# A macaron block on one core: f16 projections, stores of scores merged in pairs and issued from ACT's queue, q and k stored in one piece

## The chip, the core and the metric

The kernel runs on one core of a Trainium2 chip. The metric is the device time of one execution in microseconds (us); lower is better. A core has TensorE (PE; PEld is its loading of weights), VectorE (DVE), ScalarE (ACT), GpSimd (POOL) and SyncE (SP). Each engine carries out its instructions in the order of the program. Transfers (DMAs) are issued by an engine's queue, here that of SyncE or of ACT, and land later. "Activation" in a listing is ACT.

## What is computed

x has 8 sequences of 1024 tokens with 256 channels. Three sublayers follow one another, each with a layer norm in front and a residual:

```
x = x + 0.5 * ffn(layernorm(x))
x = x + attention(layernorm(x))
x = x + 0.5 * ffn(layernorm(x))

ffn(x):   xr, xk = mu * x + (1 - mu) * x_prev          # x_prev: the token before
          sigmoid(xr @ W_r.T) * (relu(xk @ W_k.T)**2 @ W_v.T)

attention(x), 16 heads of 16, 40 offsets o (0 to 32, 48, 64, 96, 128, 192, 256, 384):
          logit_o = (q . k shifted by o) / 4 * (1 + q . scale_o) + bias_o     # masked where t < o
          p = softmax over the offsets; out = sum over o of p_o * (v shifted by o)
          (out * gain * sigmoid(x @ gate_w.T + gate_b)) @ out_w.T + out_b
```

## The kernel before

The work is cut into five stages, written as Python generators in `macaron`: the first FFN (`stage_f1`), the projections q, k, v and gate (`stage_p`), the scores (`stage_qk`), softmax and the sum over v (`stage_att`), and the second FFN (`stage_f2`). The FFNs and projections go by 32 chunks of 256 tokens, the scores by 16 half batches of 512 tokens (four steps each), attention by 64 tiles of 128 tokens. A list of steps at the end of the function orders the stages by hand (line 520, with the offsets TRACE and RANK); within these priorities a scheduler, when the kernel is built, fixes one order of instructions for each engine. Each DMA is given one of eight completion semaphores in rotation, and is issued only when the last DMA on that semaphore has landed, if that isn't known already.

**Projections (lines 233 to 295).** The normalized chunk is transposed on TensorE and split into a high and a low part (xh, xl, lines 244 and 245), as are the weights (wa_hi, wa_lo, lines 97 to 99), all in the type F32R. Each product is three matmuls: high x high, high x low, low x high. There are 1536 of them, of 256 columns each, 48 a chunk. For q and k, ACT writes the f16 high part of the result into hl (line 263) and VectorE the low part (line 264). hl goes to DRAM twice (line 270), since the score matmul contracts over four stacked pieces: q as high, low, high, low and k as high, high, low, low. That is 2 DMAs for each of 128 tiles of hl.

**Scores (lines 297 to 367).** q and k come back from DRAM as qst and kb (lines 317 and 319). `scores` multiplies them into one PSUM bank and ACT copies the bank to SBUF, into a tile called sl (line 308). *Far* tiles, for offsets over 32, come first: two in an even half batch, four in an odd one. They go to the DRAM buffer sf (line 346), four DMAs a tile. Then come four *local* tiles, which go to the DRAM buffer of the half batch, again four DMAs a tile (line 362). In all that makes 192 + 256 = 448 DMAs of about 128 KB, from 112 tiles. The SBUF tiles come from a pool of two. All these DMAs are issued by SyncE.

**Attention (lines 369 to 506).** SyncE loads a tile's local scores from DRAM with a skew, so that each token's 33 offsets lie side by side, into lg (line 377), and the far ones into ef (line 379). VectorE multiplies them with 1 + q . scale (lines 405 and 410; the product gp is in PSUM), POOL adds the bias (line 419), ACT takes the exponential (line 425). ACT's queue stores the probabilities to DRAM (line 426), and SyncE loads them back unskewed into pd (line 428). pd is transposed on TensorE (line 464), copied to ptt by ACT (line 470) and multiplied with v.

Of the kernel before, what the change touches and what calls it, by code (L numbers as in the profile page):

```python
# [7 lines left out]

F32 = mybir.dt.float32
F32R = mybir.dt.float32r  # L10
F16 = mybir.dt.float16
I32 = mybir.dt.int32
AF = mybir.ActivationFunctionType
ALU = mybir.AluOpType
# [11 lines left out]
NL = LW + 1  # L26
# [6 lines left out]
ROW = 1024  # L33
# [4 lines left out]
VPAD = 96  # L38
VROW = 2 * 8 * 17
F2A = 28  # L40
TRACE = (0, 3.6, -4.4, -8.1, -10.6)
RANK = (0, 5.1, -4.4, -8.1, -10.6)

# [6 lines left out]
def macaron(ctx: ExitStack, tc: tile.TileContext, x, wffn, watt, wo, cols, rows, pbias, se, mask, out):  # L50
# [13 lines left out]
    bv, bo = row[:, 0], row[:, 1]  # L64
    bias = const.tile([128, NO * 16], F32, name="bias")
    msk = const.tile([128, 3, NO], F32, name="msk")
    wa_hi = const.tile([128, 4, 2, 256], F32R, name="wa_hi")
    wa_lo = const.tile([128, 4, 2, 256], F32R, name="wa_lo")
    seb = const.tile([128, 2, NO], F16, name="seb")
    half = const.tile([128, 4], F32, name="half")  # L70
    nc.gpsimd.memset(half, -0.5)
# [21 lines left out]
    def load_att():  # L93
        with tc.tile_pool(name="setup", bufs=1) as sp:
            wst = sp.tile([128, 4, 2, 256], F32, name="wst")
            nc.sync.dma_start(wst, watt.rearrange("w (c p) d -> p w c d", p=128))
            nc.vector.tensor_scalar(wst[:, 0], wst[:, 0], 0.25, None, ALU.mult)
            nc.vector.tensor_copy(wa_hi, wst)
            nc.vector.tensor_tensor(wa_lo, wst, wa_hi.bitcast(F32), ALU.subtract)
            nc.vector.tensor_scalar(b_q, b_q, 0.25, None, ALU.mult)  # L100
            nc.vector.tensor_scalar(b_g, b_g, 0.5, None, ALU.mult)
            nc.sync.dma_start(row, rows.unsqueeze(0).to_broadcast([128, 2, 256]))
            for t in [t.bitcast(F32) for t in kb] + vw:
                nc.gpsimd.memset(t, 0.0)
            zero = kb[1].bitcast(F32).rearrange("p a b w -> p (a b w)")
            for i in range(2):
                nc.sync.dma_start(v_d[i][0 : VPAD * VROW].rearrange("(p w) -> p w", p=VPAD), zero[:VPAD, :VROW])
            nc.sync.dma_start(sf_d[0:PADF].rearrange("(p w) -> p w", p=16), zero[:16, : PADF // 16])
            for c0, c1, w in ((0, 8, 384), (8, 15, 384), (15, 16, 368)):
                o = PADF + c0 * ROW + ROW - 384  # L110
                nc.sync.dma_start(flat(sf_d, o, (SF_T, 32), (ROW, c1 - c0), (1, w)), zero[:32, : (c1 - c0) * w])
            nc.sync.dma_start(flat(pd_d, NL * 16, (4 * SKEW, 128), (SKEW, 4), (1, SKEW - NL * 16)), zero[:, : 4 * 512])
            nc.sync.dma_start(bias, pbias.to_broadcast([128, NO * 16]))
            nc.sync.dma_start(msk, mask.rearrange("t p u -> p t u"))
            nc.sync.dma_start(wot, wo.rearrange("(c p) d -> p c d", p=128))
            for c in range(2):
                nc.vector.tensor_scalar(wot[:, c], wot[:, c], gain[:, c : c + 1], 0.5, ALU.mult, ALU.mult)
# [115 lines left out]
    def stage_p():  # L233
        for c in range(NCH):
# [7 lines left out]
            xh = pw.tile([128, 2, 256], F32R, name="xh", tag="xk" + s)  # L242
            xl = pw.tile([128, 2, 256], F32R, name="xl", tag="xr" + s)
            nc.scalar.copy(xh, tr)
            nc.vector.tensor_tensor(xl, tr, xh.bitcast(F32), ALU.subtract)

            def proj(w):
                p = ps.tile([128, 2, 256], F32, name="p", tag="ps" + s)
# [9 lines left out]

            for j, bb in ((0, b_q), (1, b_k)):
                p = proj(j)  # L260
                for g in range(2):
                    hl = pw.tile([128, 2, 256], F16, name="hl", bufs=4)
                    nc.scalar.activation(hl[:, 0], p[:, g], AF.Identity, bias=bb[:, g : g + 1])  # L263
                    nc.vector.scalar_tensor_tensor(  # L264
                        hl[:, 1], p[:, g], bb[:, g : g + 1], hl[:, 0], ALU.add, ALU.subtract
                    )
                    o = g * 128 * 2048 + cq * 256
                    for r in range(2):
                        ro, s2 = (r * 1024, 512) if j == 0 else (r * 512, 1024)
                        nc.sync.dma_start(flat(qk_d[i % 2][j], o + ro, (2048, 128), (s2, 2), (1, 256)), hl)  # L270
            p = proj(3)
            for g in range(2):
                nc.scalar.activation(gt[:, g], p[:, g], AF.Tanh, bias=b_g[:, g : g + 1], scale=0.5)
# [23 lines left out]
    def stage_qk():  # L297
        def scores(o, g, q4, q, k, keys):

            p = ps.tile([128, 512], F32, name="p", tag="psq")  # L300
            for pr in range(4):
                for s in range(len(q4(0))):
                    for a in range(4):
                        pp = p[32 * a : 32 * a + 32, pr * 128 : pr * 128 + 128].rearrange("n (h j) -> n h j", h=2)
                        w = 64 // len(q4(a))
                        ms = q4(a)[s]
                        mm(pp[:, :, s * w : s * w + w], q[:, pr, ms], k[:, pr, :, keys(ms)], True, True)
            nc.scalar.copy(o[:, :, :, g], p.rearrange("n (q h j) -> n j h q", q=4, h=2))  # L308

        for i in range(2 * B):  # L310
            hf = i % 2
# [11 lines left out]
            ns = 2 - hf  # L323
            nth = 4 // ns
            for th in range(nth):
                sf = psb.tile([128, 64, 2, 2, 4], F32, name="sl")
                for g in range(2):
                    scores(
                        sf,
                        g,  # L330
                        lambda a: [slice(c, 512, 16) for c in range((4 * th + a) * ns, (4 * th + a + 1) * ns)],
                        qs[i, g],
                        kb[g],
                        lambda ms: slice(LW + ms.start, LW + (hf + 1) * 512, 16),
                    )
                for a in range(4):
                    c = (4 * th + a) * ns
                    o = PADF + hf * 32 * SF_T + c * ROW
                    src = sf[32 * a : 32 * a + 32].rearrange("n j h g q -> n (j h g q)")
                    if hf == 0:  # L340
                        dst = flat(far, o, (SF_T, 32), (ROW, 2), (1, 512))
                        src = src.rearrange("n (s w) -> n s w", s=2)
                    else:
                        w = ROW - 16 if c == 15 else ROW
                        dst, src = flat(far, o, (SF_T, 32), (1, w)), src[:, :w]
                    nc.sync.dma_start(dst, src)
                if 2 * th + 2 == nth:
                    yield
            yield
            for t in range(4):  # L350
                sl = psb.tile([128, 64, 2, 2, 4], F32, name="sl")
                for g in range(2):
                    scores(
                        sl,
                        g,
                        lambda a: [slice(t * 128 + 32 * a, t * 128 + 32 * a + 32)],
                        qs[i, g],
                        kb[g],
                        lambda ms: slice(hf * 512 + ms.start, hf * 512 + ms.start + 64),
                    )  # L360
                for a in range(4):
                    nc.sync.dma_start(
                        flat(sl_d[i % 2], (4 * t + a) * BLK, (ROW, 32), (1, ROW)),
                        sl[32 * a : 32 * a + 32].rearrange("n j h g q -> n (j h g q)"),
                    )
                if t % 2:
                    yield

    def stage_att():
        for tt in range(B * NT):  # L370
# [27 lines left out]
            for h2 in range(2):  # L398
                gp = ps.tile([128, 64, 8], F32, name="gp")
                for g in range(2):  # L400
# [2 lines left out]
                        mm(gp[:, 0:NO, 4 * g + pr], q, seb[:, h2], True, True)  # L403
                e = slice(8 * h2, 8 * h2 + 8)
                nc.vector.scalar_tensor_tensor(
                    lg[:, 0:NL, e], gp[:, 0:NL], 1.0, lg[:, 0:NL, e], ALU.add, ALU.mult
                )
                for k0, k1 in FARG:
                    w0, w1 = (24 - FAR[k] // 16 for k in (k0, k1 - 1))
                    nc.vector.scalar_tensor_tensor(  # L410
                        lf[:, k0:k1, e],
                        gp[:, NL + k0 : NL + k1],
                        1.0,
                        ef[:, w0 : w1 + 1 : (w1 - w0) // (k1 - k0 - 1), e],
                        ALU.add,
                        ALU.mult,
# [169 lines left out]
```

## Time and profile before

| | us |
|---|---|
| median of 3 runs | 1260.52 (1255.84 to 1267.22) |
| the profiled execution, its own time | 1256.76 |
| its span, first to last instruction | 1254.0 |
| TensorE busy | 1089.2 |
| VectorE busy | 942.6 |
| GpSimd busy | 766.5 |
| ScalarE busy | 538.0 |

The profile is of one execution. Its page gives the busy time of each engine, then the chain of work that ended last, followed back from the last instruction, with the share of each engine and line in it, then groups of instructions by line, and the DMA issues. Further views list who waited for whom, the instructions of one line, and the instructions in order of time. "SPq" and "ACTq" are the instruction sequencers that issue DMAs; their work isn't counted as busy. A row such as `sl<-p` names the tile written and the tiles read. The granted clock of TensorE was 0.956 of full speed over the span. The sixteen DMA engines moved 282.88 MB at a mean of 226 GB/s.

### The profile page before, as it was taken

Reading aid. Unit: us, or ns where it says so; the run is one execution under the profiler, and the core shown is the slowest. Engines: PE = TensorE matmul, PEld = TensorE weight load, DVE = VectorE, ACT = ScalarE, POOL = GpSimd, SP = SyncE. Lnnn points to the kernel's source line nnn. Section 1 sums busy time; section 2 is a strip of 40 time slices with the busy share of each in tenths; the row PEclk is TensorE's granted clock in tenths of the full one; section 3 lists DMA queues with packets and bytes.
Section 4 is the critical chain, followed back from the end, with each engine's and each line's share of the span. In section 5 each row is a group of like instructions: output and inputs, shape, how many; then the busy total and the mean of one; then the engine's idle time right before and its main releaser. Section 6 shows DMA issues by size and latency. Waiting matters only on the chain.

```text
span 1254.0 us, 34712 instructions
## 1 busy us (share of the span) xinstructions
PE 1089.2 (87%) x13568; PEld 885.7 (71%) x13568; DVE 942.6 (75%) x2266; ACT 538.0 (43%) x1025; POOL 766.5 (61%) x1101
## 2 busy tenths in 40 slices
PE   2887989899799898989899989899988998888785
PEld 2676768677687677777777778786777787665664
DVE  7546768987587888879678866978858887877772
ACT  2444445344453444536345454544534444524231
POOL 7436619675575656659457564867656755657672
PEclk9999999899999999899999999999989999998988
DMA  8187888786878779787788977797787868998630
GB/s 263 32 224 222 241 242 265 229 238 194 251 226 254 230 233 274 221 252 232 193 260 257 254 201 230 228 269 227 233 243 234 269 197 254 284 280 265 202 99 24
DMA packets 256500, 282.88 MB, mean 226 GB/s; under 512 B 23440, under 2 KB 214608, under 8 KB 256336
## 3 DMA queue, kind: packets, MB, share of 16 engines
q1 hardware_dynamic: 247120, 263.36, 71.7%
q10 hardware_dynamic: 9216, 17.31, 3.8%
q8 instruction: 106, 1.74, 0.6%
q14 instruction: 58, 0.48, 0.1%
HBM read 151.67 MB, written 128.91 MB: 224 GB/s over the span
## 4 chain that ended last, share of the span: by engine, by line
PE 42%; DMA 25%; DVE 14%; SPq 6%; POOL 5%; issue 5%; ACT 4%; POOLq 0%; ACTq 0%; DVEq 0%
PE p L134 29%; DMA pd<-pd 9%; PE tra L464 4%; PE pv L134 3%; PE tra L134 3%; POOL prod L445 2%; DMA lg<-sl 2%; DMA x<-in_x_dram 2%; DMA qk<-hl 2%; DMA kb<-qk 2%; DMA sl<-sl 2%; DVE prod L457 2%; DVE xk L196 1%; PE gp L134 1%; DVE mx L423 1%
## 5 line engine op out<-in xcount | busy, mean ns | idle before, releaser
L134 PEld LDWEIGHTS <-qst 128*32 128x32 f16 (+1 forms) x5120 | 157.2, 120 | 100.1 <-issue 63.5
L134 PE MATMUL p<-kb,qst 128*32 128x128 f16 (+1 forms) x4096 | 185.1, 297 | 12.7 <-ACT sl L308 8.6
L308 ACT COPY sl<-p 128x512 f32<-128x512 f32 x224 | 130.8, 584 | 144.2 <-PE p L134 123.0
L445 POOL TENSOR_TENSOR prod<-v,lg 128x256 f32<-128x256 f32 x248 | 165.5, 687 | 10.2 <-ACT lg L425 6.1
L134 PE MATMUL p<-xk,w_f 128*128 128x256 f32 x512 | 144.9, 421 | 20.0 <-DVE xk L196 11.7
L419 POOL TENSOR_TENSOR lg<-lg,bias 128x640 f32<-128x640 f32 x64 | 113.5, 1774 | 71.8 <-DVE lg L410 66.9
L213 POOL TENSOR_TENSOR x<-x,xr 128x512 f32<-128x512 f32 x64 | 88.4, 1382 | 109.0 <-DVE xr L212 94.9
L457 DVE TENSOR_TENSOR prod<-prod 128x512 f32<-128x512 f32 (+2 forms) x120 | 126.1, 1051 | 32.1 <-POOL prod L445 31.5
L464 PE MATMUL tra<-ident,pd 128*128 128x128 f32 x512 | 97.1, 313 | 58.3 <-DMA pd<-pd 54.9
L160 ACT ACTIVATE xn<-x,nb,y 128x256 f32<-128x256 f32 x192 | 110.8, 602 | 63.0 <-DVE nb L152 55.2
L134 PE MATMUL p<-w_f,xk 128*128 128x256 f32 x512 | 132.9, 400 | 1.7 <-ACT xr L206 1.3
L134 PE MATMUL p<-w_f,xr 128*128 128x256 f32 x512 | 130.4, 396 | 3.6 <-ACT xk L201 2.8
L445 POOL TENSOR_TENSOR prod<-vn,lg 128x256 f32<-128x256 f32 x144 | 96.0, 678 | 54.3 <-ACT lg L425 35.4
L134 PE MATMUL p<-xh,wa_hi 128*128 128x256 f32 x384 | 123.2, 321 | 5.6 <-DVE hl L264 4.4
L134 PEld LDWEIGHTS p<-xk,w_f 128*128 128x128 f32 x512 | 99.3, 208 | 39.8 <-issue 10.5
L470 ACT COPY ptt<-tra 128x512 f32<-128x512 f32 x128 | 74.9, 585 | 116.1 <-PE tra L464 113.0
L464 PEld LDWEIGHTS tra<-ident,pd 128*128 128x128 f32 x512 | 71.0, 197 | 73.9 <-DMA pd<-pd 68.0
L263 ACT ACTIVATE hl<-p,col 128x256 f16<-128x256 f32 x128 | 60.6, 474 | 121.1 <-PE p L134 68.6
L134 PE MATMUL p<-xh,wa_lo 128*128 128x256 f32 x384 | 111.5, 290 | 0.0
L134 PE MATMUL p<-xl,wa_hi 128*128 128x256 f32 x384 | 111.4, 290 | 0.0
L134 PEld LDWEIGHTS p<-w_f,xr 128*128 128x128 f32 x512 | 95.3, 196 | 19.4 <-ACT xk L201 5.8
L134 PEld LDWEIGHTS p<-w_f,xk 128*128 128x128 f32 x512 | 96.0, 198 | 15.9 <-issue 2.8
(82 smaller groups left out, 2394.2 us busy)
## 6 DMA issues: line engine op xcount, KB each, us to landing
qk<-hl SPq DMA_DIRECT2D x256, 128.0 KB, 3.4
sl<-sl SPq DMA_DIRECT2D x256, 128.0 KB, 3.8
pd<-pd SPq DMA_DIRECT2D x64, 512.0 KB, 4.8
sf<-sl SPq DMA_DIRECT2D x184, 128.0 KB, 3.1
vw<-vd SPq DMA_DIRECT2D x128, 136.0 KB, 4.1
v<-vd SPq DMA_DIRECT2D x64, 272.0 KB, 4.3
lg<-sl SPq DMA_DIRECT2D x64, 264.0 KB, 4.1
pd<-lg ACTq DMA_DIRECT2D x64, 264.0 KB, 3.8
```

Source lines behind the costliest of these rows:

```text
L134: nc.tensor.matmul(o, l, r, start=start, stop=stop)
L160: nc.scalar.activation(xn, x2[:, i], AF.Identity, bias=nb[:, k : k + 1], scale=y[:, k : k + 1])
L196: nc.vector.scalar_tensor_tensor(o[:, h], xr[:, h], mu[:, h : h + 1], prev[:, h], ALU.mult, ALU.add)
L213: nc.gpsimd.tensor_tensor(x2, x2, xr, ALU.add)
L263: nc.scalar.activation(hl[:, 0], p[:, g], AF.Identity, bias=bb[:, g : g + 1])
L308: nc.scalar.copy(o[:, :, :, g], p.rearrange("n (q h j) -> n j h q", q=4, h=2))
L419: nc.gpsimd.tensor_tensor(la, la, bias, ALU.add)
L423: nc.vector.tensor_reduce(mx, lg.rearrange("p u e -> p e u"), AX.X, ALU.max)
L445: nc.gpsimd.tensor_tensor(prod[:, k], shifted[k][1]()[:, :, 0:16], lf[:, k].unsqueeze(2).to_broadcast([128, 16, 16]), ALU.mult,)
L457: nc.vector.tensor_tensor(o, terms[:, 0:m], terms[:, n - m : n], ALU.add)
L464: nc.tensor.transpose(tr[:, pr * 128 : pr * 128 + 128], pd.rearrange("p (m e) -> p m e", e=8)[:, :, 4 * g + pr], ident,)
L470: nc.scalar.copy(ptt.rearrange("p q n -> p (q n)"), tr)
```

## The change

There are four parts.

1. xh, xl, wa_hi and wa_lo become f16. The weights and the biases of q, k and v are scaled by WS = 16 (the bias of the gate isn't), and the scale is taken out later: in the copy of the scores (WS**-3), in 1 + q . scale (which becomes WS + ...), in the gate's tanh, and in the output weights. The cast to wa_hi moves from VectorE to ACT.
2. hl holds each tile of q or k with its copies, four pieces of 256. ACT and VectorE write each part twice in one instruction that reads the PSUM operand twice, and one DMA stores all of it: 128 DMAs in place of 256. The pool has two of these tiles in place of four of half the size.
3. Two tiles of scores share one SBUF tile of twice the size, and are stored together by four DMAs of about 256 KB after the second: 224 DMAs in place of 448. Which columns a far tile takes is rearranged to fit. In an even half batch, both far tiles are now made in the first of the four steps.
4. These 224 DMAs are issued by ACT's queue in place of SyncE's.

The core of the diff:

```diff
-    wa_hi = const.tile([128, 4, 2, 256], F32R, name="wa_hi")
-    wa_lo = const.tile([128, 4, 2, 256], F32R, name="wa_lo")
+    wa_hi = const.tile([128, 4, 2, 256], F16, name="wa_hi")
+    wa_lo = const.tile([128, 4, 2, 256], F16, name="wa_lo")
...
-            nc.vector.tensor_scalar(wst[:, 0], wst[:, 0], 0.25, None, ALU.mult)
-            nc.vector.tensor_copy(wa_hi, wst)
-            nc.vector.tensor_tensor(wa_lo, wst, wa_hi.bitcast(F32), ALU.subtract)
-            nc.vector.tensor_scalar(b_q, b_q, 0.25, None, ALU.mult)
+            nc.vector.tensor_scalar(wst[:, 0], wst[:, 0], 0.25 * WS, None, ALU.mult)
+            nc.vector.tensor_scalar(wst[:, 1:4], wst[:, 1:4], WS, None, ALU.mult)
+            nc.scalar.copy(wa_hi, wst)
+            nc.vector.tensor_tensor(wa_lo, wst, wa_hi, ALU.subtract)
+            nc.vector.tensor_scalar(b_q, b_q, 0.25 * WS, None, ALU.mult)
+            nc.vector.tensor_scalar(b_k, b_k, WS, None, ALU.mult)
...
+            nc.vector.tensor_scalar(bv, bv, WS, None, ALU.mult)
...
-                    hl = pw.tile([128, 2, 256], F16, name="hl", bufs=4)
-                    nc.scalar.activation(hl[:, 0], p[:, g], AF.Identity, bias=bb[:, g : g + 1])
-                    nc.vector.scalar_tensor_tensor(
-                        hl[:, 1], p[:, g], bb[:, g : g + 1], hl[:, 0], ALU.add, ALU.subtract
-                    )
-                    o = g * 128 * 2048 + cq * 256
-                    for r in range(2):
-                        ro, s2 = (r * 1024, 512) if j == 0 else (r * 512, 1024)
-                        nc.sync.dma_start(flat(qk_d[i % 2][j], o + ro, (2048, 128), (s2, 2), (1, 256)), hl)
+                    hl = pw.tile([128, 2, 2, 256], F16, name="hl", bufs=2)
+                    hi, lo = (hl[:, :, 0], hl[:, :, 1]) if j == 0 else (hl[:, 0], hl[:, 1])
+                    pp = p[:, g : g + 1].to_broadcast([128, 2, 256])
+                    nc.scalar.activation(hi, pp, AF.Identity, bias=bb[:, g : g + 1])
+                    nc.vector.scalar_tensor_tensor(lo, pp, bb[:, g : g + 1], hi, ALU.add, ALU.subtract)
+                    nc.sync.dma_start(
+                        flat(qk_d[i % 2][j], g * 128 * 2048 + cq * 256, (2048, 128), (512, 4), (1, 256)),
+                        hl.rearrange("p a b n -> p (a b) n"),
+                    )
...
-            nc.scalar.copy(o[:, :, :, g], p.rearrange("n (q h j) -> n j h q", q=4, h=2))
+            nc.scalar.mul(o[:, :, :, g], p.rearrange("n (q h j) -> n j h q", q=4, h=2), WS**-3)
...
-                sf = psb.tile([128, 64, 2, 2, 4], F32, name="sl")
+                if th % 2 == 0:
+                    sf = psb.tile([128, 2, 64, 2, 2, 4], F32, name="sl")
...
+                if th % 2 == 0:
+                    continue
...
                     if hf == 0:
-                        dst = flat(far, o, (SF_T, 32), (ROW, 2), (1, 512))
-                        src = src.rearrange("n (s w) -> n s w", s=2)
+                        dst = flat(far, o, (SF_T, 32), (ROW, 4), (1, 512))
+                        src = src.rearrange("n t (s w) -> n (t s) w", s=2)
                     else:
-                        w = ROW - 16 if c == 15 else ROW
-                        dst, src = flat(far, o, (SF_T, 32), (1, w)), src[:, :w]
-                    nc.sync.dma_start(dst, src)
-                if 2 * th + 2 == nth:
+                        dst, src = flat(far, o, (SF_T, 32), (ROW, 2), (1, ROW - 16)), src[:, :, : ROW - 16]
+                    nc.scalar.dma_start(dst, src)
+                if hf and th == 1:
                     yield
+            if not hf:
+                yield
             yield
...
-                sl = psb.tile([128, 64, 2, 2, 4], F32, name="sl")
+                if t % 2 == 0:
+                    sl = psb.tile([128, 2, 64, 2, 2, 4], F32, name="sl")
...
+                if t % 2 == 0:
+                    continue
                 for a in range(4):
-                    nc.sync.dma_start(
-                        flat(sl_d[i % 2], (4 * t + a) * BLK, (ROW, 32), (1, ROW)),
-                        sl[32 * a : 32 * a + 32].rearrange("n j h g q -> n (j h g q)"),
-                    )
-                if t % 2:
-                    yield
+                    nc.scalar.dma_start(
+                        flat(sl_d[i % 2], (4 * (t - 1) + a) * BLK, (ROW, 32), (4 * BLK, 2), (1, ROW)),
+                        sl[32 * a : 32 * a + 32].rearrange("n t j h g q -> n t (j h g q)"),
+                    )
+                yield
```

More of the change, by code (lines that the diff above doesn't have):

```diff
@@ L9 @@
 F32 = mybir.dt.float32
-F32R = mybir.dt.float32r
 F16 = mybir.dt.float16
@@ L40 @@
 F2A = 28
+WS = 16.0
 TRACE = (0, 3.6, -4.4, -8.1, -10.6)
@@ L116, in load_att @@
             for c in range(2):
-                nc.vector.tensor_scalar(wot[:, c], wot[:, c], gain[:, c : c + 1], 0.5, ALU.mult, ALU.mult)
+                nc.vector.tensor_scalar(wot[:, c], wot[:, c], gain[:, c : c + 1], 0.5 / WS, ALU.mult, ALU.mult)
             se_f = sp.tile([128, NO], F32, name="se_f")
@@ L241, in stage_p @@
             tr = norm_transposed(x1[c], y, nb, 2 * k, s)
-            xh = pw.tile([128, 2, 256], F32R, name="xh", tag="xk" + s)
-            xl = pw.tile([128, 2, 256], F32R, name="xl", tag="xr" + s)
+            xh = pw.tile([128, 2, 256], F16, name="xh", tag="xh" + s)
+            xl = pw.tile([128, 2, 256], F16, name="xl", tag="xl" + s)
             nc.scalar.copy(xh, tr)
-            nc.vector.tensor_tensor(xl, tr, xh.bitcast(F32), ALU.subtract)
+            nc.vector.tensor_tensor(xl, tr, xh, ALU.subtract)
             def proj(w):
@@ L261, in stage_p @@
                 for g in range(2):
-                    hl = pw.tile([128, 2, 256], F16, name="hl", bufs=4)
-                    nc.scalar.activation(hl[:, 0], p[:, g], AF.Identity, bias=bb[:, g : g + 1])
-                    nc.vector.scalar_tensor_tensor(
-                        hl[:, 1], p[:, g], bb[:, g : g + 1], hl[:, 0], ALU.add, ALU.subtract
-                    )
-                    o = g * 128 * 2048 + cq * 256
-                    for r in range(2):
-                        ro, s2 = (r * 1024, 512) if j == 0 else (r * 512, 1024)
-                        nc.sync.dma_start(flat(qk_d[i % 2][j], o + ro, (2048, 128), (s2, 2), (1, 256)), hl)
+                    hl = pw.tile([128, 2, 2, 256], F16, name="hl", bufs=2)
[6 more added lines that the diff above has]
+                        hl.rearrange("p a b n -> p (a b) n"),
+                    )
             p = proj(3)
             for g in range(2):
-                nc.scalar.activation(gt[:, g], p[:, g], AF.Tanh, bias=b_g[:, g : g + 1], scale=0.5)
+                nc.scalar.activation(gt[:, g], p[:, g], AF.Tanh, bias=b_g[:, g : g + 1], scale=0.5 / WS)
             p = ps.tile([128, 512], F32, name="p", tag="ps" + s)
@@ L325, in stage_qk @@
             for th in range(nth):
-                sf = psb.tile([128, 64, 2, 2, 4], F32, name="sl")
+                if th % 2 == 0:
+                    sf = psb.tile([128, 2, 64, 2, 2, 4], F32, name="sl")
                 for g in range(2):
                     scores(
-                        sf,
+                        sf[:, th % 2],
                         g,
-                        lambda a: [slice(c, 512, 16) for c in range((4 * th + a) * ns, (4 * th + a + 1) * ns)],
+                        lambda a: [slice(c, 512, 16) for c in range(4 * a + th * ns, 4 * a + (th + 1) * ns)],
                         qs[i, g],
@@ L335, in stage_qk @@
                     )
+                if th % 2 == 0:
+                    continue
                 for a in range(4):
-                    c = (4 * th + a) * ns
-                    o = PADF + hf * 32 * SF_T + c * ROW
-                    src = sf[32 * a : 32 * a + 32].rearrange("n j h g q -> n (j h g q)")
+                    o = PADF + hf * 32 * SF_T + (4 * a + (th - 1) * ns) * ROW
+                    src = sf[32 * a : 32 * a + 32].rearrange("n t j h g q -> n t (j h g q)")
                     if hf == 0:
-                        dst = flat(far, o, (SF_T, 32), (ROW, 2), (1, 512))
-                        src = src.rearrange("n (s w) -> n s w", s=2)
-                    else:
-                        w = ROW - 16 if c == 15 else ROW
-                        dst, src = flat(far, o, (SF_T, 32), (1, w)), src[:, :w]
-                    nc.sync.dma_start(dst, src)
-                if 2 * th + 2 == nth:
+                        dst = flat(far, o, (SF_T, 32), (ROW, 4), (1, 512))
+                        src = src.rearrange("n t (s w) -> n (t s) w", s=2)
+                    else:
+                        dst, src = flat(far, o, (SF_T, 32), (ROW, 2), (1, ROW - 16)), src[:, :, : ROW - 16]
+                    nc.scalar.dma_start(dst, src)
+                if hf and th == 1:
                     yield
+            if not hf:
+                yield
             yield
             for t in range(4):
-                sl = psb.tile([128, 64, 2, 2, 4], F32, name="sl")
+                if t % 2 == 0:
+                    sl = psb.tile([128, 2, 64, 2, 2, 4], F32, name="sl")
                 for g in range(2):
                     scores(
-                        sl,
+                        sl[:, t % 2],
                         g,
@@ L405, in stage_att @@
                 nc.vector.scalar_tensor_tensor(
-                    lg[:, 0:NL, e], gp[:, 0:NL], 1.0, lg[:, 0:NL, e], ALU.add, ALU.mult
+                    lg[:, 0:NL, e], gp[:, 0:NL], WS, lg[:, 0:NL, e], ALU.add, ALU.mult
                 )
@@ L412, in stage_att @@
                         gp[:, NL + k0 : NL + k1],
-                        1.0,
+                        WS,
                         ef[:, w0 : w1 + 1 : (w1 - w0) // (k1 - k0 - 1), e],
```

## The prediction

> **What bounds the kernel now.** I read the page from the top, then the chain, then the waits, and last single lines of code. All sums are made against the profiled execution: 1256.76 us, of which 1254.0 are the span; the median shown is 1260.52, so 3.8 us are added at the end. A difference below about 1% is no more than a measurement of this kernel can tell from no change.
>
> ```profile
> PE 1089.2 (87%) x13568; PEld 885.7 (71%) x13568; DVE 942.6 (75%) x2266; ACT 538.0 (43%) x1025; POOL 766.5 (61%) x1101
> ...
> q1 hardware_dynamic: 247120, 263.36, 71.7%
> q10 hardware_dynamic: 9216, 17.31, 3.8%
> ...
> PE 42%; DMA 25%; DVE 14%; SPq 6%; POOL 5%; issue 5%; ACT 4%; POOLq 0%; ACTq 0%; DVEq 0%
> ```
>
> No single engine is the bound. TensorE leads, but it makes up only 42% of the chain that ended last; a quarter of that chain is transfers in flight, and 6% is SyncE's queue (SPq). ACT is busy 43% and is 4% of the chain. Nearly all transfers go by SyncE's queue (q1), few by ACT's (q10).
>
> The waits (engine, line, whom it waited for: us in total, times, longest) say where transfers hurt:
>
> ```profile
> PE tra L464 <- DMA pd<-pd: 54.9, 33, 7.2
> PE tr L162 <- ACT xn L160: 26.2, 7, 17.6
> ...
> PE p L134 <- ACT sl L308: 8.6, 9, 4.4
> ...
> PE gp L134 <- DMA qst<-qk: 3.8, 2, 2.1
> ```
>
> ```profile
> SPq L377 <- DMA sl<-sl: 47.1, 54, 3.7
> ```
>
> TensorE's waits on DMA come to 54.9 + 3.8 + 2.0 + 1.6 = 62 us. The last line matters for the merge: 54 of SyncE's 64 loads of local scores (line 377) stand at the head of the queue until a store of scores has landed, with everything behind them.
>
> **SyncE's queue** is never free. These are the issues of a store, their count, and minimum/median/maximum in ns:
>
> ```profile
> L270 SPq DMA_DIRECT2D qk<-hl x256: 359/544/1992, 52.0 to 1110.9; - x128
> ```
>
> ```profile
> L362 SPq DMA_DIRECT2D sl<-sl x256: 302/424/1777, 95.1 to 1175.0; - x128
> ```
>
> ```profile
> L426 ACTq DMA_DIRECT2D pd<-lg x64: 326/327/387, 114.3 to 1199.5; - x64
> ```
>
> Added up over the trace's records, its 1360 issues take 736 us, so of 1254 us some 518 are left, and those are blocked. Of the 736, line 270 takes 148.6, line 346 takes 98.7 and line 362 takes 125.4. The cost shows at pd, the skewed probabilities: from the landing of the store to the issue of the load that follows it, 2.5 us pass in the median and 4.2 in the mean. ACT's own issue takes 0.33 us and never stretched.
>
> **The change, part by part.**
>
> *Projections in f16 (1536 matmuls).* The page's mean of 290 to 321 ns counts the pipeline's depth; what a matmul occupies is the distance between starts:
>
> ```profile
> 602.92 0.28 PE L134 MATMUL p<-xh,wa_lo 128*128 128x256 f32 x1
> 603.04 0.28 PE L134 MATMUL p<-xh,wa_hi 128*128 128x256 f32 x1
> 603.16 0.28 PE L134 MATMUL p<-xl,wa_hi 128*128 128x256 f32 x1
> ```
>
> That is 120 ns. f32 matmuls of 256 columns are 216 ns apart and of 128 columns 109, so a pass of 256 columns costs about 108 in any type. The saving is at most 1536 x 12 = 18 us, at least 0; TensorE is 42% of the chain, so I take **-8**.
>
> *q and k written twice.* An ACT instruction of line 263 goes from 128x256 (474 ns) to 128x512; the nearest row, the ReLU from PSUM at 128x512, takes 595: 128 x 0.121 = 15.5 us. VectorE's line 264 goes from 472 to the 679 of line 212 (128x512, PSUM source): 26.5 us. DVE is busy 75% and 14% of the chain, so a fifth of its time is on the path, and of ACT's a tenth: 5 + 1.5 = **+6.5** (0 to 42). There are two buffers instead of four, so k's first evacuation must wait until q's first store has landed (3.4 us, plus queue). In the program's new order some nine other ACT instructions mostly lie between, about 5 us of cover: **+3**; without cover 2 us x 32 chunks = 64.
>
> *Start.* The weights' high half is now cast by ACT (128x2048; four times the 0.585 of a 128x512 copy is 2.3 us, where DVE's cast took 1.23), after a further scaling of 1536 columns (3 x 0.407 = 1.2) and of a row (0.3). ACT's first normalization stands behind it, and TensorE's first work, at 17.6 us, behind that: 2.3 - 1.23 + 1.5 = **+2.5**. The other scalings cost nothing: they replace an instruction one for one.
>
> *SyncE relieved.* It loses the 448 stores of scores and 128 of the 256 of q and k. The 128 left keep their bytes in one 256 KB issue, about the same 0.54 us: 69. So 736 - 98.7 - 125.4 - 148.6 + 69 = 432 us, 41% less. If lateness falls with it, 0.41 x 62 = 25 us of TensorE's waits go; a little of that is real latency: **-22**. Bounds: 0 (the time turns into blocked time, as 518 us already are) and -75 (the whole 6% of SPq).
>
> Here a rule speaks against the change. The Trainium skill ("DMA: Bandwidth & Descriptors", section "Issuing engines are not separate DMA queues") says that several issuing engines share the same DMA engines, and that spreading only saves sequencer time, usually small beside the transfer. The row says 0.50 us of issue (mean of lines 346 and 362) against 3.1 to 3.8 us to landing: small singly, but 224 us in sum on a queue without room. By the rule this term would be near 0 and the total 1299; I follow the row, but only to -22.
>
> *The stores on ACT's queue.* 56 groups of two tiles give 224 issues of 256 KB. They cost at least 0.30 us (minimum of the sf store), at most 0.61 (the kb load, with three strided dimensions on both sides); I take 0.40, between L426 and the median 0.42: 90 us. Each must also see the last user of its completion semaphore landed. In the new order the first of four stands directly behind the copy it stores in half of the cases, and the other three mostly follow at once, so ACT's engine idles 1.6 us and more, where L426's issue has another instruction running over it. Before L426's 64 issues the sequencer stood 11.2 us in sum, four times over 1 us, longest 5.9: 0.17 each, x224 = 38. Together ACT stands 128 us longer (85 to 175). Queued behind are q/k evacuations, score copies, ptt copies, ReLU and tanh, and TensorE waits for each. ACT's share of the path is a tenth of its time (12 us) at the least; everything (128) at the most. I take 18%: **+23**.
>
> *Merge.* Bytes and packet sizes stay. But the first of two tiles leaves only with the second. From the records, a local tile's first use on VectorE follows its landing by 4.1 us for the first tile of a half batch, 11.7, 12.7 and 14.6 for the other three: the first is used as soon as store (3.8) and load (4.1) let it. The second tile lands 9.8 us after the first (mean of 16). So attention starts each of 16 half batches up to 9.8 us later: 157 us if nothing gave way. Mostly it does: the second tile has 11.7 - 4.1 = 7.6 us to spare and other stages fill the engines (VectorE waits on these loads 33.6 us in all). One such shift stays at the end, plus a little: **+12**. Far scores are needed together, and cost nothing; if they didn't, 9 us more.
>
> Sum: -8 + 6.5 + 3 + 2.5 - 22 + 23 + 12 = +17. On the profiled execution 1274; on the median **1277**.
>
> **The rivals.**
>
> *ACT's queue becomes the bound.* SyncE is late; ACT's stores wait on semaphores that SyncE's transfers hold, and ACT, in order, stops everything. For it: stalls of up to 5.9 us before L426. Against: they are few, and SyncE gets faster. If half of 128 us shows instead of 23, the time is 1277 + 41, about 1315. It decides once more than a third of ACT's standing reaches TensorE.
>
> *SyncE's relief dominates* (the other sign). Loads of pd go out as soon as their store lands, 4.2 us earlier in the mean, so that of the 62 us some 50 go, and lg's loads gain what the merge cost. 1260.5 - 8 + 12 - 50 + 20 = 1235. It needs pd's lag to fall under about 1 us; from -39 us on it cancels the rest of the sum. For it: a queue full to the last microsecond on a chain with 25% DMA. Against: 518 us of it are waits for data, which stay.
>
> *Nothing reaches the path.* SyncE's time turns into waiting, ACT's 57% idle time swallows the issues, the merge is absorbed: -8 + 12 = +4, 1265. So the move of the queue would not do what it says.
>
> **How the numbers follow.** Forecast: 50%, own range 1258 to 1298; ACT's queue 20%; SyncE's relief 25%; nothing 5%. The forecast's half splits into 0.32 over 1273 (1%) and 0.18 within 1%. Slower: 0.32 + 0.20 = 0.52. Faster: 0.24 of the relief's 0.25. Within 1%: 0.18 + 0.05 + 0.01 = 0.24. The regenerated order of instructions is in no row; I put it inside these widths. From 1225 (relief at its best) to 1318 (just past ACT's case) leaves out about 2 in 10.
>
> **What would show it.** Right: projection matmuls 108 to 120 ns apart; SyncE's issues near 430 us; the lag at pd below 4.2 but not under 1 us; ACT's store issues near 90 us with waits before them; TensorE's waits on ACT above the 46 us of now; a half batch's first local tile used some 4 us after a landing that comes later. Wrong: f16 matmuls spaced well under 108; ACT's issues hidden, with TensorE's waits on ACT unchanged; TensorE's wait on pd gone or grown; a merged issue that costs twice a single one.

## The result and the profile after

The changed kernel takes 1313.03 us in the median of 4 runs (1307.81 to 1318.64), the kernel before 1260.23 beside it: a ratio of 1.041, 95% interval 1.035 to 1.048. That is 53 us slower. The forecast was 17 us slower, 1277, in a range up to 1318; so sign and range hold, and the size is three times the one forecast. The profiled execution spans 1316.9 us.

The page of the changed kernel, the same rows as before. Its chain of waits breaks off after less than a tenth of the span, so it isn't used here.

```profile
PE 1088.7 (83%) x13568; PEld 845.8 (64%) x13568; DVE 956.6 (73%) x2268; ACT 564.8 (43%) x1026; POOL 766.0 (58%) x1101
...
q1 hardware_dynamic: 221520, 204.62, 53.3%
q10 hardware_dynamic: 29184, 75.78, 19.3%
```

No engine has much more to do: TensorE 1089 us as before, VectorE +14, ACT +27. More than a quarter of the bytes (75.8 of 282.6 MB) now goes by ACT's queue (q10). The granted clock, before and after:

```profile
core 0: 1254.0 us, clock 0.956
core 0: 1316.9 us, clock 0.936
```

So TensorE's equal busy time hides two changes. The f16 matmuls are shorter: with f16 alone (e3 below) it is busy for 1070.9 us. And the clock is lower. The trace's clock record is full or half at each moment; the halves come to 171 us of the span, 113 before, and within TensorE's busy time they cost 71.7 us, 48.5 before (half of the busy time that lies in them). They follow idleness: in the 7 us before one begins TensorE is idle for 40% of the time, over the whole span for 17%. By this, part of what a wait costs comes back as slower matmuls behind it. No run varies the clock alone, so how large a part of the 53 us that is stays open. All variants below have a lower clock than the kernel before (means of their executions 0.927 to 0.947, of the kernel before beside them 0.948 to 0.950).

Since TensorE's busy time is equal, the longer span is its idle time. Its waits in the changed kernel:

```profile
PE tra L475 <- DMA pd<-pd: 42.6, 29, 5.1
PE gp L138 <- DVE lg L421: 27.3, 21, 3.6
PE p L138 <- ACT sl L313: 22.5, 22, 3.2
...
PE p L138 <- DVE hl L271: 20.4, 17, 3.7
PE p L138 <- DVE xk L200: 16.6, 15, 2.9
PE p L138 <- DMA kb<-qk: 15.3, 7, 3.7
PE pv L138 <- ACT ptt L481: 12.7, 17, 2.2
```

Added up over all rows by the engine waited for, TensorE's idle time went from 158 to 221 us: on DMA from 62.3 to 62.6, on ACT from 46 to 68, on VectorE from 46 to 88. VectorE's own wait for ACT's half of hl grew beside it, from 24.4 to 46.2 us. The wait on DMA, which was to shrink by 22, is unchanged: on the load of pd TensorE waits 12 us less, on that of kb 14 more.

The issues of the stores of scores, now on ACT, of q and k on SyncE, and of ACT's old store (count, then minimum/median/maximum in ns):

```profile
L374 ACTq DMA_DIRECT2D sl<-sl x128: 309/440/2548, 107.5 to 1230.6; - x128
```

```profile
L353 ACTq DMA_DIRECT2D sf<-sl x96: 309/574/2377, 95.5 to 1204.0; - x96
```

```profile
L272 SPq DMA_DIRECT2D qk<-hl x128: 512/549/2302, 51.3 to 1169.7; - x128
```

```profile
L437 ACTq DMA_DIRECT2D pd<-lg x64: 326/344/1654, 131.1 to 1271.3; - x64
```

The 224 stores hold ACT's queue for 159 us, 0.71 each and not 0.40. Their medians, 0.44 and 0.57, are nearer the forecast, but issues in a burst of four stretch: the first takes 0.33 us in the mean, the second 0.61, the third 0.80, the fourth 1.11, the longest 2.55. The next rows show what that does on ACT, and then on TensorE, each in order of time (start, duration, what, and in brackets the idle time before it). An evacuation is the copy of a finished PSUM bank to SBUF:

```profile
632.11 0.68 ACT L270 ACTIVATE hl<-p,col 128x512 f16<-128x512 f32 x1
632.25 7.17 ACTq L374 DMA_DIRECT2D sl<-sl  x4
639.52 0.69 ACT L270 ACTIVATE hl<-p,col 128x512 f16<-128x512 f32 x1 [6.73 <-DMA sl<-sl]
640.11 0.59 ACT L313 ACTIVATE sl<-p 128x512 f32<-128x512 f32 x1
```

```profile
629.87 0.27 PE L138 MATMUL p<-xh,wa_hi 128*128 128x256 f16 x1
629.98 0.27 PE L138 MATMUL p<-xl,wa_hi 128*128 128x256 f16 x1
...
640.75 0.62 PE L138 MATMUL p<-kb,qst 128*32 128x128 f16 x16 [3.25 <-ACT sl L313]
...
642.79 0.42 PE L138 MATMUL p<-xh,wa_hi 128*128 128x256 f16 x1
643.01 0.42 PE L138 MATMUL p<-xl,wa_hi 128*128 128x256 f16 x1
```

Four stores occupy the queue for 7.17 us, and the first evacuation behind them starts after 6.73 us of idle time. TensorE waits 3.25 us for the second, the copy of scores at 640.11. Behind that wait the projection matmuls start 0.22 us apart and not 0.11: from 639.4 to 646.2 us the clock record stands at half. This group is one of the longest; the mean group takes 3.6 us from the first issue to the end of the fourth, and ACT's idle time that ended with a DMA rose from 37 to 144 us.

### The profile page after: what moved, and what is told of

Same layout as the page of the kernel before. It is cut to its first block, busy times and chain, and to the rows that moved or that the text cites. A ratio compares the mean times of both kernels' runs of the same rounds, so it can differ in the third digit from the quotient of the medians.

```text
span 1316.9 us, 34187 instructions
## 1 busy us (share of the span) xinstructions
PE 1088.7 (83%) x13568; PEld 845.8 (64%) x13568; DVE 956.6 (73%) x2268; ACT 564.8 (43%) x1026; POOL 766.0 (58%) x1101
## 5 line engine op out<-in xcount | busy, mean ns | idle before, releaser
L138 PE MATMUL p<-kb,qst 128*32 128x128 f16 (+1 forms) x4096 | 178.8, 294 | 39.2 <-ACT sl L313 22.5
L313 ACT ACTIVATE sl<-p 128x512 f32<-128x512 f32 x224 | 133.8, 597 | 149.2 <-PE p L138 111.0
L138 PE MATMUL p<-xk,w_f 128*128 128x256 f32 x512 | 149.2, 432 | 20.2 <-DVE xk L200 16.6
L270 ACT ACTIVATE hl<-p,col 128x512 f16<-128x512 f32 x128 | 87.7, 686 | 149.9 <-PE p L138 53.7
L430 POOL TENSOR_TENSOR lg<-lg,bias 128x640 f32<-128x640 f32 x64 | 108.6, 1698 | 54.3 <-DVE lg L421 39.7
L271 DVE SCALAR_TENSOR_TENSOR hl<-p,col,hl 128x512 f16<-128x512 f32 x128 | 94.9, 741 | 50.0 <-ACT hl L270 46.2
L138 PE MATMUL p<-xh,wa_hi 128*128 128x256 f16 x384 | 110.6, 288 | 23.1 <-DVE hl L271 20.4
L211 POOL TENSOR_TENSOR xk<-xk 128x512 f32<-128x512 f32 x64 | 74.9, 1171 | 62.1 <-ACT xk L205 61.9
L138 PE MATMUL p<-xl,wa_hi 128*128 128x256 f16 x384 | 110.2, 287 | 0.0
L138 PE MATMUL p<-xh,wa_lo 128*128 128x256 f16 x384 | 110.2, 287 | 0.0
```

The lines of the kernel that those rows point to most:

```text
L138: nc.tensor.matmul(o, l, r, start=start, stop=stop)
L211: nc.gpsimd.tensor_tensor(xk, xk, xk, ALU.mult)
L270: nc.scalar.activation(hi, pp, AF.Identity, bias=bb[:, g : g + 1])
L271: nc.vector.scalar_tensor_tensor(lo, pp, bb[:, g : g + 1], hi, ALU.add, ALU.subtract)
L313: nc.scalar.mul(o[:, :, :, g], p.rearrange("n (q h j) -> n j h q", q=4, h=2), WS**-3)
L430: nc.gpsimd.tensor_tensor(la, la, bias, ALU.add)
```

## The experiments

Each was timed against the kernel before on the same chip; that had medians of 1260 to 1265 us. Ratios carry a 95% interval. My theory after the traces was that ACT's standing during the stores costs the time (A); the rival was that the merge or the double writing of q and k does (B). Theories C and D, in later expectations, are narrower forms: standing in one piece, and the late first tile. Each variant's order of instructions is scheduled anew, and that alone moved the time by up to 18 us (the nudge, below).

**What does ACT's queue cost?** First the changed kernel with its merged stores back on SyncE (e1):

```diff
-                    nc.scalar.dma_start(dst, src)
+                    nc.sync.dma_start(dst, src)
...
-                    nc.scalar.dma_start(
+                    nc.sync.dma_start(
                         flat(sl_d[i % 2], (4 * (t - 1) + a) * BLK, (ROW, 32), (4 * BLK, 2), (1, ROW)),
```

> The changed kernel with its 224 merged stores of scores issued by SyncE again, all else as changed. If ACT's standing during the issues and waits of the stores costs the time (theory A), about 40 us come back: near 1272 us, and TensorE's waits on ACT fall from 68 us to about 45. If the merge or the double writing of q and k costs it (theory B), it stays at 1300 to 1315. If SyncE's queue had been relieved to some use, it is above 1315.

1280.39 us, 1.015 (1.009 to 1.021). So 33 of the 53 us come from the queue, though some 20 stay. Its own waits of TensorE name ACT for 48.5 us, near theory A's 45. The clock of its profiled execution is 0.936 as well (means 0.940 here, 0.936 in the changed kernel), so the clock explains little of this difference.

The reverse, on the kernel before: the 448 unmerged stores by ACT and nothing else (e2).

```diff
-                    nc.sync.dma_start(dst, src)
+                    nc.scalar.dma_start(dst, src)
...
-                    nc.sync.dma_start(
+                    nc.scalar.dma_start(
                         flat(sl_d[i % 2], (4 * t + a) * BLK, (ROW, 32), (1, ROW)),
```

> The kernel before with nothing changed but the queue of the 448 unmerged stores of scores: ACT in place of SyncE. Theory A: at 0.43 us an issue ACT stands some 190 us longer, more than the 159 us of issues in the changed kernel, so 1310 us or more. Theory B: within 1% of 1260, since neither merge nor double writing is there.

1295.4, 1.028 (1.020 to 1.035): 35 us, less than theory A's 50, but theory B's "within 1%" falls. SyncE's issues dropped here from 736 to 508 us with no merge and no double writing beside it, and TensorE's waits on DMA stayed at 61.5 (62.3 before). The clock fell here too, to 0.936 in the mean.

Of these, the local stores alone (e8; the second hunk of e2's edit):

> The kernel before with the 256 local stores alone on ACT's queue, far stores on SyncE. If the cost goes with ACT's issue time (111 of the 202 us of both), 55% of the 35 us that both cost: about 1280 us. If it sits in the local stores, because attention's first tile waits for them, nearly all: 1290 or more. If in the far stores: under 1268.

1271.67, 1.007 (1.004 to 1.009): 8 us for 55% of the issue time. In proportion it would be 19, but the 11 us between lie within what the order moves. If the cost sat in the local stores, 1290 or more was expected; that falls.

Is it ACT's time? The merged stores on SyncE, with useless work on ACT in their place (e7; an output tile that nothing reads):

```diff
+                for _ in range(3):
+                    nc.scalar.copy(junk, sl.rearrange("n t j h g q -> n (t j h g q)")[:, 512:1536])
```

> The changed kernel with its merged stores on SyncE, and three useless ACT copies of 128x1024 after each pair of tiles (168 copies of about 1.04 us, 175 us of ACT time, in pieces that the scheduler sets between others); the output is untouched. If ACT's time itself is what the move cost (theory A), 1305 us or more. If it was the standing of the queue in one piece, or its waits for other queues' transfers (theory C), well under that: 1280 to 1292.

1305.67, 1.036 (1.032 to 1.040): 25 us over e1.

```profile
L382 ACT CAST junk<-sl 128x1024 f16<-128x1024 f32 x96 | 100.3, 1044 | 1.0
L356 ACT CAST junk<-sl 128x1024 f16<-128x1024 f32 x72 | 75.3, 1046 | 0.8
```

175.6 us of plain ACT work cost 25 us, a seventh, on an engine that is busy 44% of the time in e1. By this, ACT's time by itself would be worth most of the 33 us that the 164 us of added issues cost, and the 8 us between would be for standing in one piece and for waits. That is likely rather than shown: an order of instructions moves up to 18 us, and the copies also read the score tile, which may hold it longer.

**What does f16 cost or bring?** Part 1 of the change alone (e3; hl and the stores as before):

> The kernel before with the f16 projections and their scaling alone: stores of scores unmerged on SyncE, q and k stored as before. Both theories: about 1252 us (-8; between -18 and +3 with the longer start). Above 1275 would mean that f16 or the order of instructions that the scheduler makes of it costs by itself.

1261.94, 1.0002 (0.997 to 1.003): nothing, where 8 us were expected.

**What does writing q and k twice cost?** The changed kernel without it (e4; hl's loop as before):

> The changed kernel with q and k written once into four buffers and stored by 256 DMAs as before; merge and ACT's queue stay. Theory A: little comes back, about 1300 to 1313 us. Theory B in the form that the double writing costs: it falls by 20 us or more, to 1290 or below, and TensorE's wait on hl falls from 20 us to about 5.

1311.83, 1.040 (1.034 to 1.047): nothing comes back. And f16 with it, stores of scores as before (e5):

> f16 and q and k written twice and stored in one piece; stores of scores as before (unmerged, SyncE). SyncE loses 128 issues, some 70 us, and ACT gets none. If relieving SyncE is worth what I forecast (22 us for 304 us of issues less), this is 5 us under the f16-only kernel, less up to 9 us for the longer writes: 1255 to 1266 us. If relief is worth nothing and the longer writes cost their share, 1266 to 1272.

1275.34, 1.011 (1.007 to 1.014): 13 us worse than f16 alone, with 51 us of issues fewer on SyncE (727 to 676). The same with four buffers (e11):

```diff
-                    hl = pw.tile([128, 2, 2, 256], F16, name="hl", bufs=2)
+                    hl = pw.tile([128, 2, 2, 256], F16, name="hl", bufs=4)
```

> f16 and q and k written twice and stored in one piece, with four of the double buffers in place of two; stores of scores as before. If the 13 us of the double writing come from waiting for the landing of one of only two buffers (ACT waited 18.5 us on it), 1259 to 1265; if from the longer instructions on ACT and VectorE, 1272 to 1277.

1279.28, 1.014 (1.008 to 1.020): no gain from the buffers.

**What does the merge cost?** f16, SyncE, hl as before, merged stores (e9; e1 with the old loop of hl):

> f16, merged stores of scores on SyncE, q and k written and stored as before: the merge alone. The late single stores gave 1246. If half as many issues help further, 1235 to 1243; if merging is the same as late single stores, 1246; if a merged transfer of 256 KB is worse than two single ones, 1255 to 1270. The double writing, 13 us by itself, would then be the rest up to the 1280 with it.

1289.06, 1.022 (1.017 to 1.028), above every case that was expected. Against this, with the same shared tiles but single stores, is e6:

```diff
-                    nc.sync.dma_start(
-                        flat(sl_d[i % 2], (4 * (t - 1) + a) * BLK, (ROW, 32), (4 * BLK, 2), (1, ROW)),
-                        sl[32 * a : 32 * a + 32].rearrange("n t j h g q -> n t (j h g q)"),
-                    )
+                    for z in range(2):
+                        nc.sync.dma_start(
+                            flat(sl_d[i % 2], (4 * (t - 1 + z) + a) * BLK, (ROW, 32), (1, ROW)),
+                            sl[32 * a : 32 * a + 32, z].rearrange("n j h g q -> n (j h g q)"),
+                        )
```

> f16, q and k as before, two tiles of scores in one SBUF tile, 448 single stores by SyncE, but all eight of a pair only after the second tile. If the merge costs because the first tile's scores leave late (theory D), this is as slow as the merged stores on SyncE: 1272 to 1285 us. If it costs by the larger transfers themselves or by q and k, it is near the f16-only kernel: 1258 to 1266.

1245.88, 0.988 (0.985 to 0.991): faster than both kernels, and outside both cases. It didn't do what it was made for: a single store needs only its own half of the tile, and the scheduler set it early. In the trace the first local store is issued 8.2 us *before* the second tile's copy ends (mean of 16), in e9 0.8 us *after* it. So this is a test of merging after all, by 43 us. The issues of local scores in e9, then in e6:

```profile
L374 SPq DMA_DIRECT2D sl<-sl x128: 302/590/2307, 100.7 to 1204.0; - x128
```

```profile
L375 SPq DMA_DIRECT2D sl<-sl x256: 302/422/1517, 96.3 to 1158.5; - x128
```

Half the issues, but each longer. The stores of scores, far and local, take 165 us of issues in e9 for 218 in e6. Yet all of SyncE's issues together take 725 us in e9 (1136 of them) and 725 in e6 (1360), since others grew, most of all those of hl (144 to 169), whose code is the same in both: SyncE is relieved of nothing.

Is it the room? f16 alone with four single tiles in the pool (e10):

```diff
-    psb = pool("psb", 2)
+    psb = pool("psb", 4)
```

> f16 alone, with four single tiles of scores in the pool in place of two; stores go at once, as before. If the late stores won because four tiles of room part ACT's copies from the landing of stores, this is as fast or faster: 1240 to 1247. If they won by the order of the issues on SyncE, it stays at 1262.

1267.12, 1.003 (1.001 to 1.005): no. What is left of e6 over e10 is the other sharing of far columns, the far tiles in the first step, and the order of instructions.

ACT's queue on top of e6 (e12):

> The late single stores, all 448 issued by ACT's queue in place of SyncE's; otherwise the kernel that took 1246. The same step cost 35 us without f16 and pool, 33 us on the merged stores. If it is ACT's time and standing, again 30 to 40: 1276 to 1286. If the four tiles of room take it up, under 1265.

1299.72, 1.031 (1.025 to 1.037): 54 us over e6, the dearest of all moves to ACT and above both cases.

**How much does the order alone move?** The nudge shifts the priority of the score stage by 0.35 of a step: the work stays, the scheduler writes another order. On four kernels (e13 to e16):

```diff
-    RANK = (0, 5.1, -4.4, -8.1, -10.6)
+    RANK = (0, 5.1, -4.05, -8.1, -10.6)
```

> A control: the kernel before, with the score stage's priority offset moved by a third of a step (-4.4 to -4.05), which leaves all work as it is and makes the scheduler write another order of instructions. If the regenerated order moves little, 1255 to 1270 us; if it moves the time by a per cent or two by itself, anything from 1235 to 1290.

1279.27, 1.016 (1.011 to 1.022): 18 us for nothing but another order.

> The same control on the kernel with late single stores on SyncE (1246 us). If its advantage over f16 alone was the work, 1240 to 1252; if it was its order of instructions, it moves up to 1260 or more.

1249.35, 0.991 (0.988 to 0.995): 3 us.

> The same control on the merged stores on SyncE without double writing (1289 us). If the merged transfers cost, it stays at 1280 or more and about 40 us above the control with late single stores; if the order did, the two come within 15 us of each other.

1278.58, 1.015 (1.009 to 1.021): 10 us less than e9. Merging costs 29 us under the nudge, 43 without.

> The same control on the changed kernel (1313 us). If its loss is the work, it stays 45 us or more above the nudged kernel before; if the order made half of it, about 1285.

1314.65, 1.045 (1.039 to 1.050): 2 us. Above the nudged kernel before it is 35 us, between the two cases of the expectation. So a difference of up to 18 us, the largest of these four, says little between two of these kernels. The queue's cost, 33, 23, 35 and 54 us in the four pairs that move all stores of scores, is above that.

**Delay or size?** If the first local tile's delay is the cost of the merge, merging the far stores alone (e17: e6 with e9's far stores) is harmless and merging the local ones alone (e18) is not.

> The kernel with single stores from shared tiles (1246 and, nudged, 1249 us), with its far scores merged in pairs and its local ones single, all on SyncE. In that kernel the local stores were not late after all: the trace has them issued 8 us before the second tile's copy ends, while the merged ones leave 1 us after it. If the merge costs by delaying attention's first local tile, the far merge is harmless: 1240 to 1258 us. If the 256 KB transfers cost by themselves, 1262 to 1275. The order of instructions alone moved 3 to 18 us.

1273.34, 1.011 (1.007 to 1.014): 27 us over e6.

> The complement: far scores single, local scores merged in pairs, all on SyncE. If the delay of the first local tile costs, this bears nearly the whole loss of the two merges together, 29 to 43 us: 1274 to 1290. If the size of the transfers costs, a bit over half of it: 1262 to 1272.

1269.51, 1.007 (1.004 to 1.010): 24 us over e6. Both cost, about alike. The delay can't be the cause of the far merge's, so that theory falls as the whole explanation. The size fits the even split, but as the order of instructions is worth up to 18 us, it isn't shown either. This stays open.

## Why the prediction was wrong, point by point

Sizes on the way from before to after, by the runs:

| step of the sum | forecast | measured |
|---|---|---|
| f16 and start (e3) | -8 + 2.5 | 0 (-4 to +4) |
| q and k twice (e5, e11, e1 against e9, after against e4) | +9.5 | +13, +17, -9, +1 |
| merge, on SyncE (e9 against e6; nudged; e1 against e5) | +12 | +43; +29; +5 |
| move to ACT (after against e1; e4 against e9; e2; e12 against e6) | +23 - 22 = +1 | +33; +23; +35; +54 |

*SyncE relieved, -22: this step failed.* It priced the queue's lateness as if it came from issue time. SyncE's issues did fall, to 481 us (432 forecast), but its blocked time rose from 518 to 835; from the landing of pd's store to the issue of its load 4.2 us pass in the mean, as before; TensorE's wait on DMA is 62.6 for 62.3. In e2, with 228 us fewer issues and nothing else changed, it is the same. (Against e1, 77 us, it is 14 lower; but the nudge alone moves this sum by up to 29, from 104 in e9 to 75.) The queue is blocked by data and buffers at its head, as these waits of SyncE show, first before, then in the changed kernel:

```profile
SPq L270 <- DVE hl L264: 24.1, 18, 6.0
SPq L391 <- POOL prod L445: 27.2, 21, 6.8
```

```profile
SPq L272 <- DVE hl L271: 93.8, 44, 8.5
SPq L402 <- POOL prod L456: 88.0, 36, 8.8
```

The zero bound that I had named ("the time turns into blocked time") was the answer, and the rule of the Trainium skill that I set aside ("DMA: Bandwidth & Descriptors", section "Issuing engines are not separate DMA queues": several issuing engines save only sequencer time) gave the nearer total: 1299 against 1277.

*The stores on ACT's queue, +23.* The direction and the mechanism hold: TensorE's waits on ACT rose by 21 us, and the share of ACT's time that reaches the end, 18% in the forecast, is 14% by the filler. *The time was undersized, the second step that failed:* 159 us of issues for 90, since the price came from issues that don't come four at a time. The waits before them, added up in the same way as in the forecast, are 38 us, as forecast. So ACT stood 197 us longer and not 128, past the range of 85 to 175. The 33 us over e1 are 17% of that; e4 over e9 and e2 give 11%, e12 16%. With the relief at 0 and 18% of 197 us, 35, the sum would have come to 1277 + 22 + 12 = 1311. That this meets the 1313 measured is partly luck, as the other terms are off in both directions. TensorE's waits on VectorE, +42 us, were not in the sum at all. With the stores back on SyncE (e1) they are 57 us and not 88, so the move raises them too; but the nudged kernel before has 74, so how much of them is the order's isn't known.

*Merge, +12.* Undersized too in two of three pairs, and for a cause that I can't name. The sum held the delay of the first local tile; the runs allow no such limit, since the far merge, priced at nothing, cost 27. The sign that I listed against the forecast, a merged issue that costs twice a single one, came only half way: 0.76 us (mean in e1) for 0.50.

*q and k twice.* The instructions were a little longer than forecast: 686 ns on ACT for 595, 741 on VectorE for 679. The buffers were right to cost little (e11). Beyond that the four measurements disagree in sign within the order's spread, so the +9.5 is neither confirmed nor refuted.

*f16 and start.* The matmuls are 109 ns apart. The forecast's 108 was half of f32's 216, an assumption that no row of before shows. It came true for f16, but not "in any type", as F32R's 120 shows. The saving reached TensorE's busy time, 1070.9 us in e3 for 1089.2, but not the end: the wait for pd rose from 54.9 to 80.0. The clock, for which the sum had no term, also fell: 0.939 over e3's 12 executions, 0.950 of the kernel before beside them. I estimate that at 13 us of full speed (0.0103 of 1262). TensorE's first work came 1.2 us later in the changed kernel, at 18.8, not 2.5.

*The rivals.* ACT's queue as the bound was to give 1315 (its own sum, 1277 + 41, is 1318), at 20%. The number fits, and so does its sign, stalls of several us before other evacuations. Its threshold doesn't: it asked that more than a third of ACT's standing reach TensorE, and the four pairs that move all stores show 11 to 17% (e8: 3%); a longer standing and the lack of relief did the rest. The relief as the winner, 25%, is refuted: every move to ACT made the kernel slower. Whether some relief hides in that net cost stays open, as TensorE's waits on DMA fell in two pairs (e1 to the changed kernel, e9 to e4), stayed in e2 and rose by 24 us from e6 to e12.

That the order of instructions sits "inside these widths" was true of the runs, but at up to 18 us it is as large as the forecast itself.

## What to carry to other kernels

A queue that is never idle is not yet a queue that is short of issue time: separate its issue time from its blocked time, and take credit for fewer issues only where the blocked time is small. An issue put on a compute engine stood in that engine's way in full here, at the price of bursts and not of a lone issue. ACT, busy 43% of the time, passed on 11 to 17% of its standing when it issued all stores of scores; the way that the trace shows is TensorE's and VectorE's waits for its evacuations. Read the granted clock beside the busy time: equal busy times can hide less work at a slower clock. Where a scheduler writes the order anew for each edit, measure a nudge that leaves the work as it is before reading anything into 1%: of all versions the only one that beat the kernel before, and did so under the nudge too, is f16 with single stores from shared tiles on SyncE (1246 and 1249 us, 0.988 and 0.991).

## What was not expected of the hardware

Stores of scores, four in a row on ACT's queue, took from 0.31 us (minimum) to 2.55 us an issue, and ACT's lone store, never over 0.39 us before, reached 1.65 with them around. On SyncE merging two 128 KB stores into one of 256 KB took 53 us from the stores' own issues (218 to 165) and left the sum of all its issues at 725 us. Stretches of half clock began where TensorE had been idle for 40% of the 7 us before. In the changed kernel they took 23 us more of its busy time than in the kernel before (71.7 for 48.5), more than the 18 us that f16 alone had saved.
